# Attention of a gated cross-attention block: heads in fours, and one pipeline over all batches

## The chip, the core and the metric

The kernel runs on one core of one Trainium2 chip. Its engines work side by side, each on its own queue of instructions in order, and wait for one another through semaphores: TensorE (PE in the profile, its weight loads PEld), VectorE (DVE), ScalarE (ACT), GpSimd (POOL), and SyncE (SP), which here only issues DMAs. Matmuls write into PSUM, which has eight banks of 128 x 2 KB here; DVE and ACT read them out into SBUF. The metric is the device time of the whole program in microseconds. Where a profile is shown, its own execution's time is named, since times differ by some tenths of a per cent from run to run.

## The reference

Inputs are x and a context ctx, each of 8 batches x 256 rows x 512 columns in fp32, a mask (8 x 256 x 256, all zeros in these inputs, but added all the same), two scalar gates and the weights. Cut to what matters:

```python
def w8a8_linear(x, w, b):                  # rows of x and of w rounded to whole numbers of +-127
    qx, sx = dyn_quant(x); qw, sw = quant_weight(w)
    return einsum('bnc,oc->bno', qx, qw) * (sx * sw) + b

def xattn(x, cond, mask):                  # 16 heads of 32 columns
    q = heads(w8a8_linear(x, wq, bq)); k = heads(cond @ wk.T + bk); v = heads(cond @ wv.T + bv)
    scores = einsum('bhnd,bhld->bhnl', q, k) / sqrt(32) + mask
    o = einsum('bhnl,bhld->bhnd', softmax(scores), v)
    return w8a8_linear(concat(o), wo, bo)

x = x + tanh(g_xattn) * xattn(layernorm(x), ctx, mask)
x = x + tanh(g_ffn) * ffn(layernorm(x))    # fp8 gate, up (1408 wide) and down, columns reordered by two lists
```

The FFN rounds its weights and its input rows to an fp8 grid, after the columns are picked by a list of indices; a column that the list leaves out does not count for the row's largest value.

## The kernel before, in words

Rows lie on the 128 partitions: a batch has 2 tiles of 128 rows (TPB = 2), 2 tiles of context rows (LC = 2), and the 512 columns are 4 blocks of 128 (KC = 4), each of which holds 4 heads of 32 (HPC = 4).

Start: weights wk and wv are transposed (prep_fp32), wq and wo rounded and transposed (prep_int8), batch 0 is normalised and its q, k and v are made. mark_held writes two tables in DRAM (which columns the lists hold) by a chain of DMAs on POOL; load_held (L337) reads them back as mu_b and md_b.

The attention part, lines 187 to 762, runs batch by batch. For batch b, `attention` (L499) walks 11 steps over the batch's 8 pairs of heads:

- scores(i) (L518): for the pair (2i, 2i+1) four matmuls of 32 x 128 by 32 x 256 (two row tiles x two heads, L525), issued so that the heads alternate. A head's 32 rows of q and k lie on partitions 0, 32, 64 or 96 on, so the two heads use two row groups of TensorE's array. Each fp32 matmul stands in the profile as two passes. The results fill the tile s, two banks, of which there is one (ps_s, bufs=1). Then DVE adds the mask, turns the sign and takes the row minimum (L540, sn and nm), and ACT takes the exponential with its row sum (L550, pr).
- transposed(i) (L560), one step later: each head's pr is transposed by four matmuls against the identity (L566) into the tile t (one bank, ps_t, bufs=2), which DVE (even heads, L575) or ACT (odd heads, L573) copies out as pT.
- weighted and normalised (L578, L596), after every second pair: pT times v for four heads, in four column groups (L584, tile poT, ps_o, one bank), ACT's copy oT (L598), two transposes (L601, po), and the division by the row sums on DVE (L607).

Besides these, `attention` is given a list of other steps, handed out evenly over its 11 steps in the order of the list: for batch 0 the layer norm's statistics of the other 14 row tiles (norm_steps) and out_scales; for the others first the last batch's project_out (L630: absmax of o, rounding, transposes, matmuls with wo at L654, x updated on POOL at L665 and L666) and quantise_x2 (L670: the FFN's input rounded, transposed to x2T, and stored to DRAM on SP, L693); then the next batch's project_kv (L406: context transposed to cT, keys L424, values L438) and project_q (L452); then its share of the 29 weight pieces (prep_up L344: an indirect load on POOL, a multiplication by mu_b on POOL at L352, an absmax on DVE, rounding, transposes; prep_down; and the gathers by index). All these take their PSUM banks from a third pool (ps_m, three banks, helper `bank`). load_batch (L398) issues the next batch's context and mask loads on SP.

The order on each engine is not the order of the code. A scheduler at compile time plays the program through with modelled durations: each engine takes, among the instructions that are ready in its model, the one that stands first in the program. The order that comes out is fixed; on the chip each engine then works through its queue in order. So where a step is handed out sets its rank, not its place, and an instruction whose inputs come later than in the model holds up all behind it on its engine. A tile is allocated when a buffer of its tag is free.

After batch 7 its project_out and quantise_x2 follow alone, and then the FFN over 16 row tiles (from L766), which the change does not touch.

Of the kernel before, what the change touches and what calls it, by code (L numbers as in the profile page):

```python
# [29 lines left out]
F32 = mybir.dt.float32  # L30
BF16 = mybir.dt.bfloat16
# [9 lines left out]
P = 128  # L41
# [10 lines left out]
def tile_flamingo_block(  # L52
# [26 lines left out]
    H = 16  # L79
# [6 lines left out]
    HPC = P // D  # L86
    ISD = float(1.0 / (D ** 0.5))
# [98 lines left out]
    with ExitStack() as actx:  # L186
# [8 lines left out]
        ps_t = actx.enter_context(tc.tile_pool(name="ps_t", bufs=2, space=PSUM))  # L195
        ps_o = actx.enter_context(tc.tile_pool(name="ps_o", bufs=1, space=PSUM))
        ps_m = actx.enter_context(tc.tile_pool(name="ps_m", bufs=3, space=PSUM))

        def bank(name, dt=F32):
            n = 512 if dt == F32 else 1024  # L200
            return ps_m.tile([P, n], dt, tag="m", name=name)
# [204 lines left out]
        def project_kv(b, cr):  # L406
            cT = ld.tile([P, KC, L], F32, tag="cT", name=f"cT_{b}", bufs=1)
            kT = kv.tile([P, KC, L], F32, tag="kT", name=f"kT_{b}")
            v = kv.tile([P, LC, C], F32, tag="v", name=f"v_{b}")
# [25 lines left out]
            def values(lt):  # L435
                pv = bank(f"pv_{b}_{lt}")
# [8 lines left out]
                nc.vector.tensor_tensor(v[:, lt, :], pv, bv_b, ALU.add)  # L445
# [53 lines left out]
        def attention(b, qT, kT, v, mk, others):  # L499
# [8 lines left out]
            NP = H // 2  # L508
            PPC = HPC // 2

# [7 lines left out]
            def scores(i):  # L518
                heads = (2 * i, 2 * i + 1)
                both = ps_s.tile([P, 2, TPB, L], F32, tag="s", name=f"s_{b}_{i}")  # L520
                pss = {h: both[:, h % 2] for h in heads}

                def product(nt, h):
                    oc, r0 = h // HPC, (h % HPC) * D
# [9 lines left out]
                for h in heads:  # L534
                    sn = at.tile([P, TPB, L], F32, tag="sn", name=f"sn_{b}_{h}")
                    pr = at.tile([P, TPB, L], F32, tag="pr", name=f"pr_{b}_{h}", bufs=4)
# [23 lines left out]
            def transposed(i):  # L560
                for h in (2 * i, 2 * i + 1):
                    pr = probs.pop(h)
                    pst = ps_t.tile([P, LC, S], F32, tag="t", name=f"t_{b}_{h}")
# [14 lines left out]
            def weighted(oc):  # L578
                heads = range((oc + 1) * HPC - 1, oc * HPC - 1, -1)
                poT[oc] = ps_o.tile([P, S], F32, tag="o", name=f"poT_{b}_{oc}")  # L580

                def product(lc, h):
# [3 lines left out]
                        v[:, lc, h * D : (h + 1) * D],  # L586
# [9 lines left out]
            def normalised(oc):  # L596
                oT = at.tile([P, S], F32, tag="oT", name=f"oT_{b}_{oc}")
# [16 lines left out]
            last = NP + 2  # L614
            given = 0
            for i in range(last + 1):
                if i < NP:
                    scores(i)
                if 0 <= i - 1 < NP:
                    transposed(i - 1)  # L620
                if 0 <= i - 2 < NP and (i - 2) % PPC == PPC - 1:
                    weighted((i - 2) // PPC)
                    normalised((i - 2) // PPC)
                upto = len(others) * (i + 1) // (last + 1)
                for f in others[given:upto]:
                    f()
                given = upto
            return o
# [41 lines left out]
        def quantise_x2(b):  # L670

            xT = at.tile([P, KC, S], BF16, tag="x2T", name=f"x2T_{b}")
# [29 lines left out]
        rows_q = load_rows("q", wq, "pr", 4)  # L702
# [36 lines left out]
        start = norm_steps(TPB, NT) + [out_scales]  # L739
# [195 lines left out]
```

## Time and profile before

| | us |
|---|---|
| time, median of 3 runs | 778.96 (775.64 to 783.07) |
| the profiled execution's own time | 773.38 |
| its span (first to last instruction) | 771.6 |
| PE busy / DVE / ACT / POOL | 580.6 / 534.6 / 417.8 / 278.0 |
| first scores of batch 0; of batch 1; last scores of batch 7 | 35.5; 123.2; ends 514.3 |
| mean granted TensorE clock | 0.855 |

How to read the profile: "busy" is the time in which an engine had at least one instruction at work. A group is all instructions of one line, engine and tile; its columns are the number, the time that they cover, the mean of one, and the idle time of the engine just ahead of them with what ended it. A name like s<-kT,qT is output and inputs by the program's names. The granted clock is the share of full speed that TensorE got; it is either 1.0 or 0.5 at any one time, so a mean of 0.8 is 40% of the time at half speed. A wait for several things is put down to the one that came last. Times of a stretch are in us from the span's start.

### The profile page before, as it was taken

The numbers are of one execution on the slowest core, as the hardware profiler recorded it, in microseconds if no ns is written. First come the engines' busy times: TensorE is split into PE (matmuls) and PEld (weight loads), VectorE is DVE, ScalarE is ACT, GpSimd is POOL, SyncE is SP. The second block draws the span as 40 slices with busy tenths as digits, with TensorE's granted clock in tenths as the row PEclk, the third lists the DMA queues.
The fourth block names the chain that finished last, engine by engine and source line by source line (L and its number), as shares of the span: only waits on it lengthen the run. The fifth ranks groups of instructions, "written<-read, shape, count | busy, mean of one in ns | idle before, by whom it ended". The sixth has DMA issues, their size and how long they took to land. (4 is left out here: it accounts for less than half of the span.)

```text
span 771.6 us, 10456 instructions
## 1 busy us (share of the span) xinstructions
PE 580.6 (75%) x3584; PEld 364.4 (47%) x3584; DVE 534.6 (69%) x1421; ACT 417.8 (54%) x965; POOL 278.0 (36%) x241
## 2 busy tenths in 40 slices
PE   3852697797897797897898896765577768678762
PEld 3631465464555465654565564442354334344431
DVE  2953867957848748858857768865477777868971
ACT  3532954756756656765855666643244444445550
POOL 3623342152132242142114100060654666555440
PEclk9985888999899799799897797595698899989985
DMA  9811041030113130120114011230100101000000
GB/s 289 274 11 14 6 139 28 3 93 15 42 51 108 49 96 15 41 66 5 42 28 147 4 52 41 76 111 14 55 11 18 41 28 38 31 28 28 29 14 27
DMA packets 27157, 42.59 MB, mean 55 GB/s; under 512 B 6528, under 2 KB 14080, under 8 KB 27104
## 3 DMA queue, kind: packets, MB, share of 16 engines
q1 hardware_dynamic: 18656, 29.17, 11.2%
q0 software_dynamic: 4864, 12.22, 5.9%
q10 hardware_dynamic: 3584, 0.54, 0.4%
q8 instruction: 28, 0.46, 0.2%
q14 instruction: 25, 0.20, 0.1%
HBM read 31.28 MB, written 10.63 MB: 54 GB/s over the span
## 5 line engine op out<-in xcount | busy, mean ns | idle before, releaser
L550 ACT ACTIVATE pr<-sn,nm 128x256 f32<-128x256 f32 x256 | 127.6, 501 | 82.6 <-DVE nm L540 81.9
L525 PE MATMUL s<-kT,qT 32*128 32x256 f32 x512 | 88.5, 471 | 57.2 <-DVE nm L540 52.2
L540 DVE CUSTOM_DVE_ANT_0 sn<-s,mk 128x256 f32<-128x256 f32 x256 | 97.0, 418 | 14.4 <-PE s L525 14.4
L566 PE MATMUL t<-ident,pr 128*128 128x128 f32 x512 | 93.8, 323 | 15.9 <-DVE mv L679 6.7
L525 PEld LDWEIGHTS s<-kT,qT 32*128 32x128 f32 x512 | 52.9, 221 | 85.2 <-DVE nm L540 53.8
L566 PEld LDWEIGHTS t<-ident,pr 128*128 128x128 f32 x512 | 67.7, 164 | 43.9 <-ACT pr L550 22.1
L825 PEld LDWEIGHTS <-xg 128*128 128x128 bf16 x512 | 52.7, 104 | 74.6 <-issue 34.7
L857 POOL TENSOR_TENSOR tt<-up,sl 128x704 f32<-128x704 f32 x32 | 62.9, 1966 | 39.5 <-DVE up L847 23.8
L825 PE MATMUL p_up<-upT,xg 128*128 128x352 bf16 x256 | 52.0, 341 | 20.9 <-DVE up L847 18.2
L424 PE MATMUL pk<-cT,wkT 128*128 128x256 f32 x256 | 60.1, 391 | 3.2 <-ACT cT L417 3.0
L825 PE MATMUL p_gate<-gateT,xg 128*128 128x352 bf16 x256 | 48.9, 335 | 14.2 <-DVE gs L838 7.5
L665 POOL TENSOR_TENSOR x_sb<-x_sb,bo_b 128x512 f32<-128x512 f32 x16 | 22.4, 1406 | 97.8 <-ACT xq L462 97.8
L438 PE MATMUL pv<-wvT,cT 128*128 128x512 f32 x128 | 56.5, 594 | 0.0
L424 PEld LDWEIGHTS pk<-cT,wkT 128*128 128x128 f32 x256 | 48.8, 195 | 12.1 <-ACT cT L417 5.8
L666 POOL TENSOR_TENSOR x_sb<-x_sb,y 128x512 f32<-128x512 f32 x16 | 20.1, 1267 | 89.4 <-DVE y L662 89.3
L184 DVE TENSOR_REDUCE mxt<-tt 128x1 f32<-128x1408 f32 x16 | 25.9, 1620 | 33.6 <-POOL tt L857 33.6
L550 ACT ACTIVATION_READ_ACCUMULATOR pr<-sn,nm 128x1 f32 x256 | 48.7, 190 | 0.0
L493 POOL TENSOR_SCALAR qT<-qT,bq_c 128x256 f32<-128x256 f32 x32 | 19.4, 618 | 80.1 <-DVE qT L490 80.0
L875 PE MATMUL yp<-wdT,qtT 128*128 128x512 bf16 x176 | 44.7, 408 | 2.9 <-ACT qtT L872 2.9
L872 ACT COPY qtT<-ptq 128x1024 bf16<-128x1024 bf16 (+1 forms) x32 | 22.3, 749 | 43.0 <-PE ptq L869 43.0
L162 ACT ACTIVATE v_t<-tt,rs_t 128x1408 f32<-128x1408 f32 x16 | 23.5, 1469 | 39.9 <-DVE sy L879 39.9
L575 DVE COPY pT<-t 128x512 f32<-128x512 f32 x64 | 43.7, 682 | 1.6 <-PE t L566 1.0
(184 smaller groups left out, 1183.6 us busy)
## 6 DMA issues: line engine op xcount, KB each, us to landing
cr<-in_ctx_dram SPq DMA_DIRECT2D x8, 512.0 KB, 3.8
x_sb<-in_x_dram SPq DMA_DIRECT2D x8, 512.0 KB, 9.0
out_dram<-yo SPq DMA_DIRECT2D x16, 256.0 KB, 2.0
wd<-in_L_ffn_w_down_dram SPq DMA_DIRECT2D x4, 704.0 KB, 4.1
mk<-in_mask_BxSxS_ff_dram SPq DMA_DIRECT2D x8, 256.0 KB, 2.7
scr_x<-x2T SPq DMA_DIRECT2D x8, 256.0 KB, 3.1
scr_gate<-gateT SPq DMA_DIRECT2D x1, 1408.0 KB, 5.5
scr_up<-upT SPq DMA_DIRECT2D x1, 1408.0 KB, 5.1
```

Of the source, the lines that this page charges most:

```text
L162: nc.scalar.activation(v, src, AF.Identity, scale=rs)
L184: nc.vector.tensor_reduce(dst, src, AX.X, ALU.max, apply_absolute_value=True)
L424: nc.tensor.matmul(pk[:, :L], wTf["k"][:, cc, oc * P : (oc + 1) * P], cT[:, cc, :], start=(cc == 0), stop=(cc == KC - 1),)
L438: nc.tensor.matmul(pv, cT[:, cc, lt * P : (lt + 1) * P], wTf["v"][:, cc, :], start=(cc == 0), stop=(cc == KC - 1),)
L525: return nc.tensor.matmul(pss[h][:, nt, :], qT[r0 : r0 + D, oc, nt * P : (nt + 1) * P], kT[r0 : r0 + D, oc, :], start=True, stop=True,)
L540: nc.vector.tensor_tensor_reduce(out=sn[:, nt, :], in0=pss[h][:, nt, :], in1=mk[:, nt, :], scale=-1.0, scalar=3.0e38, op0=ALU.add, op1=ALU ...
L550: nc.scalar.activation(pr[:, nt, :], sn[:, nt, :], AF.Exp, bias=nm[:, nt : nt + 1], scale=-1.0, accum_out=sums[:, nt, h : h + 1],)
L566: nc.tensor.transpose(pst[:, lc, nt * P : (nt + 1) * P], pr[:, nt, lc * P : (lc + 1) * P], ident,)
L575: nc.vector.tensor_copy(pT, pst)
L825: nc.tensor.matmul(ph[n][:, j, :QI], xg[:, k, nt * P : (nt + 1) * P], wT[n][:, k, c0 : c0 + QI], start=(k == 0), stop=(k == KC - 1),)
L857: nc.gpsimd.tensor_tensor(tt[:, cols], up, sl, ALU.mult)
L875: nc.tensor.matmul(py, qT[:, k, :], wdT[:, k, :], start=(k == 0), stop=(k == IC - 1))
```

## The change

Three things are changed in the attention part.

1. scores works on four heads at a time. For even i it issues the eight matmuls of one column block, heads in turn (four row groups), into one tile s of four banks, of which there is again one; then the eight row minima and exponentials. For odd i it does nothing. pr gets six buffers instead of four.
2. ps_t, ps_o and ps_m become one pool of four banks, from which t, poT, po and all other steps take theirs.
3. The walk over steps leaves `attention`, which now returns its three stages. One loop runs over all 64 pairs, with the pairs' transposes one pair later and the products two pairs later also across the border of two batches. The other steps of a batch are put into eight slots, one per pair, by kind: `spread` divides each list over a stretch of slots. v's tile is allocated at its first use; oT and x2T move to a pool with one buffer.

The core of the diff (where a tile's pool alone changes, and where v becomes a list of one, is left out):

```diff
-        ps_t = actx.enter_context(tc.tile_pool(name="ps_t", bufs=2, space=PSUM))
-        ps_o = actx.enter_context(tc.tile_pool(name="ps_o", bufs=1, space=PSUM))
-        ps_m = actx.enter_context(tc.tile_pool(name="ps_m", bufs=3, space=PSUM))
+        ps_m = actx.enter_context(tc.tile_pool(name="ps_m", bufs=4, space=PSUM))
...
             def scores(i):
-                heads = (2 * i, 2 * i + 1)
-                both = ps_s.tile([P, 2, TPB, L], F32, tag="s", name=f"s_{b}_{i}")
-                pss = {h: both[:, h % 2] for h in heads}
+                if i % PPC:
+                    return
+                oc = i // PPC
+                heads = range(oc * HPC, (oc + 1) * HPC)
+                four = ps_s.tile([P, HPC, TPB, L], F32, tag="s", name=f"s_{b}_{oc}")
+                pss = {h: four[:, h % HPC] for h in heads}
...
-                    pr = at.tile([P, TPB, L], F32, tag="pr", name=f"pr_{b}_{h}", bufs=4)
+                    pr = at.tile([P, TPB, L], F32, tag="pr", name=f"pr_{b}_{h}", bufs=6)
...
-                    pst = ps_t.tile([P, LC, S], F32, tag="t", name=f"t_{b}_{h}")
+                    pst = bank(f"t_{b}_{h}").rearrange("p (c n) -> p c n", n=S)
...
-                poT[oc] = ps_o.tile([P, S], F32, tag="o", name=f"poT_{b}_{oc}")
+                poT[oc] = bank(f"poT_{b}_{oc}")[:, :S]
...
-            last = NP + 2
-            given = 0
-            for i in range(last + 1):
-                if i < NP:
-                    scores(i)
-                if 0 <= i - 1 < NP:
-                    transposed(i - 1)
-                if 0 <= i - 2 < NP and (i - 2) % PPC == PPC - 1:
-                    weighted((i - 2) // PPC)
-                    normalised((i - 2) // PPC)
-                upto = len(others) * (i + 1) // (last + 1)
-                for f in others[given:upto]:
-                    f()
-                given = upto
-            return o
+            def products(i):
+                if i % PPC == PPC - 1:
+                    weighted(i // PPC)
+                    normalised(i // PPC)
+
+            return o, (scores, transposed, products)
...
-        after = start
-        for b in range(B):
-            n0, n1 = (len(pieces) * i // (B - 1) for i in (b, b + 1))
-            others = after + pieces[n0:n1]
-            if b + 1 < B:
-                cr, mk_next = load_batch(b + 1)
-                kT_next, v_next, kv_steps = project_kv(b + 1, cr)
-                qT_next, q_steps = project_q(b + 1)
-                others = after + kv_steps + q_steps + pieces[n0:n1]
-            o = attention(b, qT, kT, v, mk, others)
-            after = project_out(b, o) + quantise_x2(b)
-            if b + 1 < B:
-                qT, kT, v, mk = qT_next, kT_next, v_next, mk_next
-        for f in after:
-            f()
+        def spread(slots, steps, first, end):
+            for k, f in enumerate(steps):
+                slots[first + k * (end - first) // len(steps)].append(f)
+
+        parts = {}
+        for g in range(B * NP + NP):
+            b, i = divmod(g, NP)
+            if i == 0:
+                slots = [[] for _ in range(NP)]
+                if b < B:
+                    o, parts[b] = attention(b, qT, kT, v, mk)
+                if b == 0:
+                    spread(slots, norm_steps(TPB, NT), 0, 4)
+                    spread(slots, [out_scales], 5, 6)
+                if b + 1 < B:
+                    cr, mk = load_batch(b + 1)
+                    kT, v, kv_steps = project_kv(b + 1, cr)
+                    qT, q_steps = project_q(b + 1)
+                    spread(slots, kv_steps, 0, 6)
+                    spread(slots, q_steps, 4 if b == 0 else 3, 7)
+                if b > 0:
+                    spread(slots, project_out(b - 1, o_last) + quantise_x2(b - 1), 2, NP)
+                if b < B - 1:
+                    n0, n1 = (len(pieces) * k // (B - 1) for k in (b, b + 1))
+                    spread(slots, pieces[n0:n1], 4 if b == 0 else 0, NP)
+                o_last = o
+            for lag in range(3):
+                if 0 <= g - lag < B * NP:
+                    parts[(g - lag) // NP][lag]((g - lag) % NP)
+            for f in slots[i]:
+                f()
```

More of the change, by code (lines that the diff above doesn't have):

```diff
@@ L86, in tile_flamingo_block @@
     HPC = P // D
+    NP = H // 2
+    PPC = HPC // 2
     ISD = float(1.0 / (D ** 0.5))
@@ L408, in project_kv @@
             kT = kv.tile([P, KC, L], F32, tag="kT", name=f"kT_{b}")
-            v = kv.tile([P, LC, C], F32, tag="v", name=f"v_{b}")
+            v = []
             def transposed(lt):
@@ L435, in values @@
             def values(lt):
+                if lt == 0:
+                    v.append(kv.tile([P, LC, C], F32, tag="v", name=f"v_{b}"))
                 pv = bank(f"pv_{b}_{lt}")
@@ L444, in values @@
                     )
-                nc.vector.tensor_tensor(v[:, lt, :], pv, bv_b, ALU.add)
+                nc.vector.tensor_tensor(v[0][:, lt, :], pv, bv_b, ALU.add)
             steps = [partial(transposed, lt) for lt in range(LC)]
@@ L497, in project_q, with attention @@
             return qT, [rows] + [partial(queries, oc) for oc in range(KC)]
-        def attention(b, qT, kT, v, mk, others):
+        def attention(b, qT, kT, v, mk):
             o = kv.tile([P, TPB, C], F32, tag="o", name=f"o_{b}")
@@ L507, in attention @@
             probs, probsT, poT = {}, {}, {}
-            NP = H // 2
-            PPC = HPC // 2
             def in_turn(products):
@@ L518, in scores @@
             def scores(i):
-                heads = (2 * i, 2 * i + 1)
-                both = ps_s.tile([P, 2, TPB, L], F32, tag="s", name=f"s_{b}_{i}")
-                pss = {h: both[:, h % 2] for h in heads}
+                if i % PPC:
[4 more added lines that the diff above has]
+                pss = {h: four[:, h % HPC] for h in heads}
                 def product(nt, h):
-                    oc, r0 = h // HPC, (h % HPC) * D
+                    r0 = (h % HPC) * D
                     return nc.tensor.matmul(
@@ L585, in product @@
                         poT[oc][r0 : r0 + D, :],
-                        v[:, lc, h * D : (h + 1) * D],
+                        v[0][:, lc, h * D : (h + 1) * D],
                         probsT[h][:, lc, :],
@@ L596, in normalised @@
             def normalised(oc):
-                oT = at.tile([P, S], F32, tag="oT", name=f"oT_{b}_{oc}")
+                oT = one.tile([P, S], F32, tag="oT", name=f"oT_{b}_{oc}")
                 nc.scalar.copy(oT, poT.pop(oc))
@@ L670, in quantise_x2 @@
         def quantise_x2(b):
-            xT = at.tile([P, KC, S], BF16, tag="x2T", name=f"x2T_{b}")
+            xT = one.tile([P, KC, S], BF16, tag="x2T", name=f"x2T_{b}")
             def rows(nt):
@@ L701, in tile_flamingo_block @@
         rows_v = load_rows("v", wv, "pT", 6)
-        rows_q = load_rows("q", wq, "pr", 4)
+        rows_q = load_rows("q", wq, "pr", 6)
         two = one.tile([P, 2, C], F32, tag="wd", name="wr_o01")
@@ L738, in tile_flamingo_block @@
         so_b = wp.tile([P, C], F32, tag="so_b", name="so_b")
-        start = norm_steps(TPB, NT) + [out_scales]
         pieces = [partial(prep_up, "gate", w_gate, k) for k in range(IC)]
```

## The prediction

> **What bounds the kernel now.** I read the page first, then the time by stage, then who waits for whom, then single stretches in order of time. The page names the costliest groups; columns after the bar are busy time, mean ns of one, then idle time of the engine just before.
>
> ```profile
> PE 580.6 (75%) x3584; PEld 364.4 (47%) x3584; DVE 534.6 (69%) x1421; ACT 417.8 (54%) x965; POOL 278.0 (36%) x241
> ...
> L550 ACT ACTIVATE pr<-sn,nm 128x256 f32<-128x256 f32 x256 | 127.6, 501 | 82.6 <-DVE nm L540 81.9
> L525 PE MATMUL s<-kT,qT 32*128 32x256 f32 x512 | 88.5, 471 | 57.2 <-DVE nm L540 52.2
> L540 DVE CUSTOM_DVE_ANT_0 sn<-s,mk 128x256 f32<-128x256 f32 x256 | 97.0, 418 | 14.4 <-PE s L525 14.4
> ```
>
> 75% for PE is an average. By the starts of the score matmuls (L525) the eight batches begin at 35.5, 123.2, 179.4, 236.1, 295.1, 351.5, 407.4 and 469.1 us, and the last scores end at 514.3; then comes a tail, and the FFN from about 545. Batches 1 to 6 take 345.9 us, 57.65 each. I cut each of them in two and asked for the busy time by stretch (columns: stretch, length, busy of PE, PEld, DVE, ACT, POOL with counts, granted clock, DMA share, GB/s):
>
> ```profile
> 179.40:206.00 26.60, 19.87 (x136) 12.22 (x132) 21.89 (x73) 16.31 (x48) 4.40 (x4) 0.81 0.00 1
> 206.00:236.10 30.10, 29.03 (x194) 19.53 (x193) 18.24 (x66) 19.62 (x55) 10.58 (x11) 1.00 0.20 62
> ...
> 295.10:322.00 26.90, 21.83 (x141) 13.52 (x138) 22.54 (x77) 16.89 (x48) 4.40 (x4) 0.75 0.00 1
> 322.00:351.50 29.50, 28.36 (x190) 18.95 (x187) 18.83 (x66) 20.13 (x56) 12.77 (x13) 1.00 0.24 72
> ```
>
> Every batch has a first half in which DVE is the fuller engine (over the six: DVE 142 of 173 us, PE 131, at granted clocks of 0.72 to 0.87), because the steps given first are the last batch's output projection and x2 quantising; and a second half that is PE alone (166 of 173 us, DVE 105), because the k, v and q projections of the next batch come there in one lump. So PE bounds half of each batch, and an alternation of PE and DVE the other half. In full-clock time a batch's PE work is about 44.4 us: in the first halves the mean clock of 0.80 means 69 of 173 us at half speed, PE busy through most of them, so some 30 of its 131 us are lost to it: (131 - 30 + 166) / 6. DVE has 247 / 6 = 41.2 us, ACT 36.5.
>
> Batch 0 is longer, 87.8 us, for one wait:
>
> ```profile
> PE s L525 <- DVE nm L540: 52.2, 22, 22.4
> ...
> DVE mx_gate L184 <- POOL wr_gate L352: 30.4, 6, 21.3
> ```
>
> Columns: us in total, times, longest. DVE stands 21.3 us (48.8 to 70.1) at an absmax of a gate weight tile, whose multiplication by mu_b on POOL waits for the table of held indices; the scores behind it on DVE wait too, so PE's 22.4 us is the same stall. Without it PE's wait for nm is 29.8 us over 21 times.
>
> **Part 1: four heads in turn.** How much a row group costs is seen where other matmuls run side by side (start, length):
>
> ```profile
> 213.36 1.07 PE L584 MATMUL poT<-pT,v 128*32 128x256 f32 x16
> 214.36 1.13 PE L525 MATMUL s<-kT,qT 32*128 32x256 f32 x8
> 215.48 0.44 PE L601 MATMUL po<-ident,oT 128*128 128x128 f32 x2
> 215.76 3.62 PE L424 MATMUL pk<-cT,wkT 128*128 128x256 f32 x16
> ```
>
> A 256-column fp32 pass alone costs about 0.22 us (pk: 16 in 3.62). A pair's eight passes in two row groups take 1.13, so two run at once (0.11 each); the sixteen passes of poT, in four column groups, take 1.07. Scores of a quad are sixteen passes. Nothing in the trace shows four row groups; ends: as poT 1.07 us, no better than two groups 2.0 us (0.38 + 15 x 0.108), one after another 3.6 us. I take 1.13, nearest to poT, the one row with four parts of the array. 64 pairs x 1.13 become 32 quads x 1.13: 36 us less PE work at full clock, 44 of the 88.5 measured, 4.5 us per batch. At 2.0 it is 8 us less; at 3.6, 43 us more. PE work of a batch falls to 39.9, beside DVE's 41.2: the late one after this is DVE.
>
> The wait that comes with it: the tile s keeps one buffer, now of four banks, so the next quad waits for all eight sn of this one. In batches 2 to 6 I paired first matmul and last reader of each bank: a pair holds its two for 4.2 us (write 1.4, wait 0.9, read 2.0). A quad: 1.4 + 0.9 + about 4, at ACT's pace, since sn has two buffers and exponentials follow at 0.49 us (72.50, 73.01, 73.50 in the trace). 6.3 of some 13 us per quad: it fits, priced at nothing while other work stands ahead on PE; with none, 6.3 - 4.2 = 2 us each, 64 us in all.
>
> **Part 2: four banks for all else, six before.** The same pairing over 179 to 469 us gives 633 us of holds, 2.18 banks on average; more than four are held 2% of the time, 6 us. Ends: nothing, and the second rival's price. I take nothing.
>
> **Part 3: one pipeline.** No instruction is added; the same steps are handed out over eight pair slots: k/v in slots 0 to 5, output projection and x2 in 2 to 7, q from 3, weight pieces across all, where before they came in that lumped order. PE's full half and DVE's full half then lie over each other. Floor: the larger of 39.9 and 41.2. Before, 57.65 against a largest engine of 44.4 is 77%; three engines at 36 to 41 in one stretch, with in-order queues, should not do much better: 80% of 41.2 gives 51.5 us per batch. Ends: only part 1 counts (57.65 - 4.5, or 53), and 48.5 (85%). Moved with the steps are their queues: weight pieces put an indirect load and a 1.27 us multiplication on POOL (busy 92 of 346 us in these batches), cr and mk loads and the x2T stores go through SP, where a cr load already waits up to 46 us for the last cT without anyone waiting for it; x2T and oT with one buffer wait for a store (3.1 us) and two transposes (0.44), a batch and a quad earlier. All priced at nothing; uncovered, the store costs 3 us a batch.
>
> Batches 1 to 6: 6 x 6.15 = 37 us less.
>
> **Batch 0, batch 7, tail.** Batch 0's stall has its cause in a chain of POOL DMAs that the change does not touch, so it stays; but the k, v and q work of batch 1, which now fills 101 to 123 (PE 20.6 of 22.2 us, DVE 13.9), can go beside the DVE-bound pairs (DVE 23.5 of 28.8 us at 72 to 101). DVE works 52.8 us of the 66.5 outside the stall; I take 8 of that 13.7, ends 0 and 30 (with the stall filled). Batch 7 has no next batch: DVE 38.5 of 45.2 us, so 3 of its 5.5 us of halved scores. The tail 514 to 545, the last x2 chain, and the FFN are unchanged.
>
> **Sum**: 37 + 8 + 3 = 48 us from the profiled execution's 773.4 (span 771.6), 725. The median shown is 779, 0.7% above it; scaled, **730 us**.
>
> **Rivals.**
> A, better than that: the k/v work fills the stall and the six batches reach 48.5: 55 + 20 + 3 = 78, scaled 700. For it: the clock was 1.00 in every half where PE was full but one (0.97), so denser PE may lose no clock. Against: DVE would be busy 85%.
> B, only two row groups run at once: parts 2 and 3 alone, some 54.5 per batch, 19 + 8 + 1 = 28 us less, 751.
> C, the clock: granted clock is 1.00 where PE is 96% busy, 0.66 in batch 7 at 76%. If spreading leaves PE everywhere at 80% and the clock goes to 0.80, PE needs 39.9 / 0.8 = 50, with 6 us idle 56 per batch: 18 us less, 760 to 775. Against: the half-clock stretches follow stretches of idle PE, which spreading removes. The Trainium skill, TensorE: Matmul & The Clock Gate, Part 1, says that the clock is halved by default and released by activity in a window of about 3.4 us; by that rule shorter scores could cost clock, and the trace's 0.66 in batch 7 agrees.
> D, slower: banks. A quad makes eight exponentials in a row, 4 us on ACT instead of 2, and ACT takes half of the t copies and all of cT, kT and oT. Waits of full banks double: t from 2.16 us (16 a batch), pk 1.01, poT 1.14, so a batch's holds go from 127 to 170 us. At 51.5 us that is 3.3 of four banks on average; if PE, in order, can keep only 2.7 filled, a batch takes 63: 6 x 5.3 - 11 = 21 us more, 800. It turns to slower below 2.9 banks. Against: 2.18 on average now. The Trainium skill speaks for it in TensorEngine Tiling (Array Packing), PSUM Bottleneck: tiling speeds TensorE but not PSUM's emptying, which may become the limit.
>
> **Chances.** Forecast 0.48, A 0.16, B 0.06, C 0.10 (half of it within 1%), D 0.20. A measurement of this kernel can tell about 1%, 8 us. Faster by more: 0.48 + 0.16 + 0.06 + 0.05 = 0.75; within: 0.05; slower: 0.20. The range runs from half of A, 698, to 790, which leaves out D's most and A's best.
>
> **What would show it.** Scores: 16 records in about 1.13 us, L525 near 44 us busy. Batch starts some 51 us apart; DVE over 78% busy in them, PE no longer at 96% in second halves; the stall before mx_gate still near 21 us. Wrong if score passes take 2 us or more per quad, if PE's waits before t, pk or pv name copies on ACT or DVE (D), if its wait for nm, outside the stall, rises from 30 to over 60 us, or if the clock falls under 0.85 in batches 1 to 6 (C).

## The result, and the profile after

The changed kernel takes **753.35 us** (median of 4 runs, 752.33 to 754.75) against 781.02 for the kernel before (4 runs, 775.64 to 783.25): a ratio of 0.9657 with a 95% interval of 0.9599 to 0.9714. So it is faster by 3.4%, where 730 us, 6.3% less than the median then known, was forecast. The profiled execution has a span of 751.4 us, against 771.6 before. The terms below are compared by these two spans, since only they can be cut into stages; they are 20.2 us apart, the medians 27.7, so the stages show some 7 us less than the whole gain.

The page of the changed kernel, same columns as before:

```profile
PE 525.7 (70%) x3561; PEld 341.6 (45%) x3584; DVE 548.2 (73%) x1429; ACT 415.0 (55%) x957; POOL 278.9 (37%) x241
...
L553 ACT ACTIVATE pr<-sn,nm 128x256 f32<-128x256 f32 x256 | 128.3, 505 | 58.1 <-DVE nm L543 45.4
L543 DVE CUSTOM_DVE_ANT_0 sn<-s,mk 128x256 f32<-128x256 f32 x256 | 98.4, 416 | 13.8 <-PE s L528 5.5
...
L528 PE MATMUL s<-kT,qT 32*128 32x256 f32 x512 | 41.3, 433 | 9.3 <-DVE nm L543 7.9
```

The scores (L528 now) are busy 41.3 us instead of 88.5, and TensorE's idle time ahead of them is 9.3 us instead of 57.2. ACT's idle time ahead of its exponentials is 58.1 us instead of 82.6, DVE's ahead of sn hardly less (13.8, before 14.4). On TensorE those are 47 and 48 us; the span fell by 20. Where the rest went is read from the stages. Cut at the first score matmul of each batch, the last stage ending with the first FFN matmul (us):

| | batch 0 | 1 | 2 | 3 | 4 | 5 | 6 | 7 and tail |
|---|---|---|---|---|---|---|---|---|
| before | 87.7 | 56.2 | 56.7 | 59.0 | 56.4 | 55.9 | 61.7 | 75.0 |
| after | 80.5 | 49.3 | 52.0 | 52.9 | 51.3 | 50.4 | 63.6 | 86.7 |

At the start of batch 6 the changed kernel is 35 us ahead. It gives 1.9 back in batch 6 and 11.7 behind it. The busy time by stretch of the changed kernel, batches 1, 5 and 6, then batch 7 up to its last scores, then the tail (columns as in the prediction; batches 2 to 4 are like 5):

```profile
116.30:165.60 49.30, 36.50 (x294) 25.42 (x294) 41.64 (x131) 31.57 (x90) 18.11 (x17) 0.93 0.14 42
...
321.80:372.20 50.40, 41.91 (x327) 28.37 (x324) 43.06 (x145) 36.25 (x101) 12.40 (x12) 0.94 0.14 44
372.20:435.80 63.60, 45.41 (x320) 31.79 (x318) 53.07 (x151) 43.42 (x114) 11.65 (x12) 0.85 0.23 75
435.80:486.00 50.20, 36.18 (x275) 23.86 (x276) 31.05 (x101) 26.32 (x81) 13.42 (x15) 0.77 0.21 64
486.00:522.50 36.50, 13.92 (x88) 8.08 (x87) 20.43 (x63) 11.30 (x29) 5.11 (x5) 0.70 0.03 10
```

Batches 1 to 5 have one pattern: DVE is the fullest engine (81 to 85% of the stretch), PE a little under it, the clock at 0.91 to 0.94. Batch 6 has 10 us more of DVE than its neighbours, and 63.60 - 53.07 = 10.5 us without DVE, about as many as they have (7.3 to 10.0). After it the engines are emptier: DVE 62% in batch 7, 56% in the tail.

Two stretches of the trace show what is in the two places. First DVE in batch 6, the lines that take the absmax of a row tile of w_down (start, length):

```profile
372.79 1.61 DVE L186 TENSOR_REDUCE mx_d<-wd 128x1 f32<-128x1408 f32 x1
...
396.89 1.61 DVE L186 TENSOR_REDUCE mx_d<-wd 128x1 f32<-128x1408 f32 x1
...
411.12 1.61 DVE L186 TENSOR_REDUCE mx_d<-wd 128x1 f32<-128x1408 f32 x1
...
428.44 1.61 DVE L186 TENSOR_REDUCE mx_d<-wd 128x1 f32<-128x1408 f32 x1
```

All four prep_down pieces, the last of the 29 but for a gather, have their absmax in batch 6. Before the change the absmaxes stood at 435.9, 456.8, 475.3 and 487.3 us: two in batch 6 (407 to 469), two in batch 7. Then TensorE at the end of batch 7, in order of time (in brackets the idle time just before, and what ended it):

```profile
484.87 1.15 PE L528 MATMUL s<-kT,qT 32*128 32x256 f32 x16
...
492.10 0.61 PE L281 MATMUL tb_x<-ident_b,q 128*128 128x128 bf16 x4 [5.72 <-DVE q L169]
492.50 1.91 PE L569 MATMUL t<-ident,pr 128*128 128x128 f32 x8
...
499.81 0.61 PE L281 MATMUL tb_x<-ident_b,q 128*128 128x128 bf16 x4 [5.39 <-DVE q L169]
500.21 1.91 PE L569 MATMUL t<-ident,pr 128*128 128x128 f32 x8
```

tb_x are the x2 transposes of batch 6. They stand in TensorE's queue ahead of transposes of the last two quads, and TensorE stands 5.72 and 5.39 us for them; behind them come the last products, the projection of batch 7 and the FFN. From the last scores to the FFN it takes 36.5 us, before 29.8.

Last, the waits of the changed kernel (total, times, longest):

```profile
DVE mx_gate L186 <- POOL wr_gate L352: 24.3, 1, 24.3
PE t L569 <- DVE woT L284: 23.6, 1, 23.6
...
PE s L528 <- DVE nm L543: 7.9, 3, 3.3
...
DVE sn L543 <- PE s L528: 5.5, 7, 1.9
```

The stall of batch 0 is still there, 24.3 us (21.3 before), and TensorE's 23.6 is the same stall under another name. The wait for nm, which a quad might have made worse, is 7.9 us in all. DVE's wait for scores is 5.5 us, before 14.4.

### The profile page after: what moved, and what is told of

It reads as the page before. It is cut to its first block, busy times and chain, and to the rows that moved or that the text cites. A ratio compares the mean times of both kernels' runs of the same rounds, so it can differ in the third digit from the quotient of the medians.

```text
span 751.4 us, 10398 instructions
## 1 busy us (share of the span) xinstructions
PE 525.7 (70%) x3561; PEld 341.6 (45%) x3584; DVE 548.2 (73%) x1429; ACT 415.0 (55%) x957; POOL 278.9 (37%) x241
## 5 line engine op out<-in xcount | busy, mean ns | idle before, releaser
L553 ACT ACTIVATE pr<-sn,nm 128x256 f32<-128x256 f32 x256 | 128.3, 505 | 58.1 <-DVE nm L543 45.4
L543 DVE CUSTOM_DVE_ANT_0 sn<-s,mk 128x256 f32<-128x256 f32 x256 | 98.4, 416 | 13.8 <-PE s L528 5.5
L569 PE MATMUL t<-ident,pr 128*128 128x128 f32 x512 | 83.6, 314 | 26.6 <-DVE woT L284 23.6
L569 PEld LDWEIGHTS t<-ident,pr 128*128 128x128 f32 x512 | 69.4, 164 | 31.6 <-DVE woT L284 23.8
L424 PE MATMUL pk<-cT,wkT 128*128 128x256 f32 x256 | 64.1, 403 | 2.4 <-issue 2.4
L836 PE MATMUL p_gate<-gateT,xg 128*128 128x352 bf16 x256 | 49.2, 337 | 14.7 <-DVE gs L849 7.9
L440 PE MATMUL pv<-wvT,cT 128*128 128x512 f32 x128 | 58.6, 603 | 0.0
L424 PEld LDWEIGHTS pk<-cT,wkT 128*128 128x128 f32 x256 | 50.7, 205 | 9.7 <-issue 2.7
L528 PE MATMUL s<-kT,qT 32*128 32x256 f32 x512 | 41.3, 433 | 9.3 <-DVE nm L543 7.9
L576 ACT COPY pT<-t 128x512 f32<-128x512 f32 x64 | 37.0, 578 | 18.7 <-PE t L569 14.0
L886 PE MATMUL yp<-wdT,qtT 128*128 128x512 bf16 x161 | 42.6, 413 | 5.1 <-ACT qtT L883 3.1
L587 PE MATMUL poT<-pT,v 128*32 128x256 f32 x512 | 41.4, 450 | 2.0 <-DVE pT L578 1.0
L893 POOL TENSOR_TENSOR yo<-yo,x_sb 128x512 f32<-128x512 f32 x16 | 21.6, 1347 | 53.7 <-issue 44.3
```

The source lines that it names most:

```text
L424: nc.tensor.matmul(pk[:, :L], wTf["k"][:, cc, oc * P : (oc + 1) * P], cT[:, cc, :], start=(cc == 0), stop=(cc == KC - 1),)
L440: nc.tensor.matmul(pv, cT[:, cc, lt * P : (lt + 1) * P], wTf["v"][:, cc, :], start=(cc == 0), stop=(cc == KC - 1),)
L528: return nc.tensor.matmul(pss[h][:, nt, :], qT[r0 : r0 + D, oc, nt * P : (nt + 1) * P], kT[r0 : r0 + D, oc, :], start=True, stop=True,)
L543: nc.vector.tensor_tensor_reduce(out=sn[:, nt, :], in0=pss[h][:, nt, :], in1=mk[:, nt, :], scale=-1.0, scalar=3.0e38, op0=ALU.add, op1=ALU ...
L553: nc.scalar.activation(pr[:, nt, :], sn[:, nt, :], AF.Exp, bias=nm[:, nt : nt + 1], scale=-1.0, accum_out=sums[:, nt, h : h + 1],)
L569: nc.tensor.transpose(pst[:, lc, nt * P : (nt + 1) * P], pr[:, nt, lc * P : (lc + 1) * P], ident,)
```

## The experiments

My theory after this: halved score time and the spread order are worth some 5.6 us in each of batches 1 to 5; the end gives back 14, because work was spread to where it stands in the way. The rival: scores and the pipeline bring little each, and something else (buffers, banks, order by chance) made the gain. I first took the change apart, then priced the score time by itself, then went at the end. Two kernels repeat score matmuls, which is said there; no kernel leaves work out.

### What the parts do alone

**Part 3 without part 1.** The changed kernel with pairs of heads again, one score tile of two banks, and six banks in the common pool:

```diff
-        ps_m = actx.enter_context(tc.tile_pool(name="ps_m", bufs=4, space=PSUM))
+        ps_m = actx.enter_context(tc.tile_pool(name="ps_m", bufs=6, space=PSUM))
...
-                if i % PPC:
-                    return
                 oc = i // PPC
-                heads = range(oc * HPC, (oc + 1) * HPC)
-                four = ps_s.tile([P, HPC, TPB, L], F32, tag="s", name=f"s_{b}_{oc}")
-                pss = {h: four[:, h % HPC] for h in heads}
+                heads = (2 * i, 2 * i + 1)
+                both = ps_s.tile([P, 2, TPB, L], F32, tag="s", name=f"s_{b}_{i}")
+                pss = {h: both[:, h % 2] for h in heads}
```

> The changed kernel with its one pipeline, but scores of two heads at a time as before, into two banks, and one pool of six banks for all else: part 3 of the change with a pool of six, without the quads. If the halved score work on TensorE carries the gain (44 us of its busy time), some 25 us of it come back in the batches, where DVE is now nearly as full: 770 to 785, score matmuls near 88 us busy. If the even spreading alone carries it: 750 to 760.

Measured: 782.45 us, ratio 1.0055 (1.0024 to 1.0086). With a common pool of six banks the pipeline alone gains nothing; it is half a per cent slower. (With the three old pools it was not run.) Batches 1 to 5 take 58.6 us each, against 56.8 before. Its waits:

```profile
PE s L526 <- DVE nm L541: 37.0, 10, 22.6
...
DVE sn L541 <- PE s L526: 25.7, 25, 2.3
```

22.6 of the 37.0 are the stall of batch 0. The other line has grown: DVE waits 25 times, 25.7 us, for scores that come late behind other work on TensorE, where the changed kernel has 5.5 us and the kernel before 14.4. A pair's scores are needed twice as often as a quad's, and with one tile none can be made ahead.

**Parts 1 and 2 without part 3.** Quads and the pool of four, in the old walk batch by batch with the old order of lists:

```diff
-        def spread(slots, steps, first, end):
...
+        start = norm_steps(TPB, NT) + [out_scales]
+        after = start
+        for b in range(B):
+            n0, n1 = (len(pieces) * i // (B - 1) for i in (b, b + 1))
...
+                others = after + kv_steps + q_steps + pieces[n0:n1]
+            o = attention(b, qT, kT, v, mk, others)
```

> Quads into four banks and the pool of four banks, but the walk batch by batch with the other steps in their old list order: parts 1 and 2 without part 3. TensorE's second halves get shorter by two quads' worth, the first halves, where DVE is fuller, stay: 755 to 768. If four banks are too few where the projections come in a lump: 785 or more, with waits of TensorE for copies on ACT or DVE.

Measured: 839.06 us, ratio 1.0782 (1.0749 to 1.0815): 61 us slower than the kernel before, although TensorE has less to do (555.4 us busy against 580.6). Batches 1 to 5 take 67.3 us each at a clock of 0.80. Waits of this kernel:

```profile
PE tb_x L281 <- DVE q L169: 43.8, 13, 4.5
...
PE po L604 <- ACT oT L601: 37.9, 19, 11.3
```

These are not waits for a free bank. They are engines that stand at instructions whose inputs come later than the written order supposes. So I took the pool by itself.

**Part 2 alone.** The kernel before, with t, poT and all else in one pool of four banks instead of six banks in three pools; two banks stay empty:

```diff
-        ps_t = actx.enter_context(tc.tile_pool(name="ps_t", bufs=2, space=PSUM))
-        ps_o = actx.enter_context(tc.tile_pool(name="ps_o", bufs=1, space=PSUM))
-        ps_m = actx.enter_context(tc.tile_pool(name="ps_m", bufs=3, space=PSUM))
+        ps_m = actx.enter_context(tc.tile_pool(name="ps_m", bufs=4, space=PSUM))
```

> The kernel before with t, poT, po and all else from one pool of four banks, as in the change, and nothing else changed (two banks stay unused): part 2 alone. By the holds of before (2.18 of six banks on average, over four 2% of the time): 775 to 787. If a pool of four is what made quads in the old walk slow (839): 800 to 830.

Measured: 832.39 us, ratio 1.076 (1.0698 to 1.0823). I had priced this edit at nothing, and in the old walk it costs 58 us by the medians of one chip (774.65 for the kernel before). Three lines of its waits, then the last two of them in the kernel before:

```profile
PE s L523 <- DVE nm L538: 76.4, 29, 23.7
...
DVE pT L573 <- PE t L564: 23.4, 20, 4.1
ACT pT L571 <- PE t L564: 22.7, 31, 3.1
```

```profile
ACT pT L573 <- PE t L566: 6.3, 3, 3.2
...
DVE pT L575 <- PE t L566: 1.0, 3, 0.5
```

With two banks of its own for t, TensorE transposed ahead of the copies; ACT and DVE waited 7.3 us for it in all. In the common pool they wait 46.1. Pairing first matmul and last reader of each bank says the same from the other side: a t bank is held 4.05 us before, 2.16 of it waiting for its copy, and 1.87 us, 0.45 of it waiting, in this kernel. (These are means over batches 2 to 6.) And the banks are not full: all four are held at once about 1% of the time. So it is not four banks that the chip runs out of. The order that the planner wrote for a common pool has the transposes later on TensorE's queue, just ahead of their copies. That much the holds and waits show; why the planner writes that order was not found, and whether it comes of the sharing or of the number was not run: no kernel of the old walk has six banks in one pool.

**A pool of four under the new pipeline.** Pairs again, one score tile, pool of four, two banks empty; that is the first experiment with four banks in place of six:

```diff
...
-                four = ps_s.tile([P, HPC, TPB, L], F32, tag="s", name=f"s_{b}_{oc}")
...
+                both = ps_s.tile([P, 2, TPB, L], F32, tag="s", name=f"s_{b}_{i}")
...
```

> The one pipeline, scores of two heads at a time into one tile of two banks, and the pool of four banks; two banks stay unused. Beside the run with two such tiles (742) only the second tile is missing. If the second tile, which lets scores run ahead of DVE, is what carries the gain of that run: 780 to 800, with TensorE's and DVE's waits for each other at the scores back at 40 us or more. If the order that comes with a pool of four is what carries it: 740 to 755.

Measured: 767.47 us (760.27 to 771.20), ratio 0.9882 (0.9831 to 0.9932), between the two times that I expected. Under the pipeline four shared banks do no harm against six: the ratio is 0.017 lower, about 13 us. The step that costs 58 us in the old walk, from three pools to one, was not run in the new one.

This kernel is also the fairest price of the quads, since against the changed kernel only they are missing. The ratios are 0.9882 and 0.9657, some 17 us. Batches 1 to 5 take 55.8 us against 51.2, with 9.7 us of score matmuls in each against 4.8: the saved time shows almost in full there.

**A second score tile instead of quads.** The same, with the two empty banks given to scores:

```diff
-        ps_s = actx.enter_context(tc.tile_pool(name="ps_s", bufs=1, space=PSUM))
+        ps_s = actx.enter_context(tc.tile_pool(name="ps_s", bufs=2, space=PSUM))
```

> The one pipeline with scores of two heads at a time, but two such tiles of two banks, so that the next pair's scores need not wait for DVE, and the pool of four banks: PSUM is divided as in the changed kernel, and TensorE's score time is that of before (about 84 us against 41). If score time on TensorE is what counts: 770 to 785, as with one tile and six banks. If the buffer counts: 750 to 758.

Measured: 742.01 us, ratio 0.9589 (0.9529 to 0.9648), a span of 739.7. My expectation was wrong on both of its sides. The kernel does scores in pairs, 77.0 us of TensorE instead of 41.3, and is no slower than the one with quads. Its scores on the page, and DVE's wait for them:

```profile
L526 PE MATMUL s<-kT,qT 32*128 32x256 f32 x512 | 77.0, 420 | 3.2 <-DVE nm L541 2.9
```

```profile
DVE sn L541 <- PE s L526: 3.5, 4, 1.4
```

Against the pairs with one tile, DVE's wait for scores goes from 23.1 us to 3.5, and the ratio from 0.9882 to 0.9589: scores can now be made one pair ahead. By stage it is not better than quads everywhere: batches 1 to 5 take 52.6 us each (quads 51.2), but batch 6 takes 53.1 (63.6), since more of the prep_down work falls into batch 7 (DVE there and in the tail 63.0 us, against 51.5).

Batches 1 to 5 of these kernels side by side, mean us of one, from the one profiled execution of each:

| walk | scores | banks for all else | us |
|---|---|---|---|
| old | pairs, one tile | 2 + 1 + 3 (before) | 56.8 |
| old | pairs, one tile | 4 | 66.6 |
| old | quads | 4 | 67.3 |
| new | pairs, one tile | 6 | 58.6 |
| new | pairs, one tile | 4 | 55.8 |
| new | pairs, two tiles | 4 | 52.6 |
| new | quads | 4 (after) | 51.2 |

The two kernels with pairs and one tile in the new walk differ less than the table has it: the profiled executions took 788.20 and 760.27 us, on both sides of medians of 782.45 and 767.47. No part that was run has the gain by itself, and they don't add up: part 2 loses when alone, part 3 gains nothing. Part 1 alone was not run, since its four banks and the old six are more than the eight there are. Nor were pr's six buffers in place of four, or the single buffers of oT and x2T, which every kernel of the table has but the first two.

### Does the time of the scores count?

**Two row groups at a time.** The changed kernel, its eight score matmuls issued as one pair's four and then the other pair's four:

```diff
-                in_turn([partial(product, nt, h) for nt in range(TPB) for h in heads])
+                two = (heads[:2], heads[2:])
+                in_turn([partial(product, nt, h) for hs in two for nt in range(TPB) for h in hs])
```

> The changed kernel with one line other: the eight score matmuls of a quad are issued as two pairs one after the other, so that two row groups run at a time instead of four; banks, pool, pipeline and slots stay. The sixteen passes should take about 2.0 us instead of 1.15, 27 us more of TensorE in all. If TensorE still sets the pace of the batches: 770 to 780. If DVE sets it now: 753 to 760.

Measured: 751.55 us, ratio 0.9658 (0.9603 to 0.9714), no change. But the edit did not make the scores slower, so it says nothing on what it was to decide. Its group on the page:

```profile
L528 PE MATMUL s<-kT,qT 32*128 32x256 f32 x512 | 41.5, 437 | 9.0 <-DVE nm L544 8.0
```

41.5 us busy, 41.3 in the changed kernel. The sixteen passes of a quad take 1.16 us (1.15), and start in rounds of four (in the first quad at 0, 7, 27 and 34 ns, then from 0.32 us on), though the second pair's stand behind all of the first pair's in the program. I come back to this at the end.

**Scores made twice.** The changed kernel with every score matmul issued a second time into the same place:

```diff
-                in_turn([partial(product, nt, h) for nt in range(TPB) for h in heads])
+                in_turn([partial(product, nt, h) for nt in range(TPB) for h in heads] * 2)
```

> The changed kernel with the eight score matmuls of each quad issued twice in a row into the same tile: 1.15 us more TensorE work per quad at full clock, 37 us in all, about what the change took away; nothing else is added. If the shorter scores on TensorE are what the change gains by: 770 to 785, near the run with pairs (782). If the gain is the larger score buffer, which lets DVE and ACT run on, and TensorE has slack now: 753 to 762.

Measured: 784.16 us, ratio 1.0125 (1.0072 to 1.0179). Its scores on the page and DVE's wait for them:

```profile
L528 PE MATMUL s<-kT,qT 32*128 32x256 f32 x1024 | 73.7, 430 | 8.9 <-DVE nm L543 8.8
```

```profile
DVE sn L543 <- PE s L528: 24.9, 17, 2.7
```

L528 is busy 73.7 us instead of 41.3, and the span grows from 751.4 to 781.1: 30 us for 32. That the two sums agree so well is luck, as the stages show. Batches 0 and 1 together grow by 10 us, as some of the other steps moved from batch 1 into batch 0; batches 2 to 5 grow by 8.0 us each, for 4.4 us of score time; and batch 7 with the tail falls by 13.6, from 86.7 to 73.1, in another order of the same steps. So in batches 2 to 5 longer scores cost more than their own time. DVE now waits 24.9 us for scores instead of 5.5, and the clock there is 0.87 to 0.90 instead of 0.91 to 0.94. The first experiment, pairs in place of quads (83.9 us busy), cost some 30 us by the ratios, but 13 of these belong to its six banks.

**Scores made twice, two tiles.** The same doubling of the kernel with pairs and two tiles:

> Two score tiles of two banks each and the pool of four, with the four score matmuls of each pair issued twice in a row: 1.1 us more TensorE work per pair, some 60 us in all. If TensorE's score time is hidden once scores can run ahead: 745 to 757. If TensorE is the bound also here: 780 or more, TensorE over 620 us busy.

Measured: 804.25 us (791.60 to 806.67), ratio 1.0353 (1.0305 to 1.04). The profiled execution is the one of 791.60. In it the scores go from 77.0 to 134.1 us busy, and the span from 739.7 to 789.8: 50 us for 57. By stage, batches 0 and 1 together grow by 20.1 us for 14.8 us of score time, and batches 2 to 5 by 4.6 each for 7.1. So the whole grows by nearly all that was added, but in batches 2 to 5 a third of it is hidden in this execution. DVE's wait for scores stays short (9.3 us, before the doubling 3.5).

### What the end gives back

**Weight pieces over all eight batches**, so that batch 7 has its share and batch 6 is not the last:

```diff
-                if b < B - 1:
-                    n0, n1 = (len(pieces) * k // (B - 1) for k in (b, b + 1))
+                if b < B:
+                    n0, n1 = (len(pieces) * k // B for k in (b, b + 1))
```

> The changed kernel with the 29 weight pieces divided over eight batches instead of seven, so that most of the down weights' pieces fall into batch 7, which has no next batch to project. If the 14 us that the change gives back from batch 6 on are the down weights' DVE work in the already full batch 6: 742 to 748, batch 6 near 52 us. If they are the pipeline's end or the banks: 751 to 757.

Measured: 746.91 us, ratio 0.9613 (0.9569 to 0.9657); the span is 743.7, 7.7 less than the changed kernel's. The two intervals overlap, so the whole is not surely faster; the stage is clear. Batch 6:

```profile
372.80:424.90 52.10, 40.80 (x324) 27.95 (x324) 39.50 (x135) 34.34 (x98) 12.83 (x13) 0.97 0.20 66
```

Batch 6 takes 52.1 us with 39.5 of DVE, like the others: its 63.6 came from the pieces. But batch 7 and tail take 89.8 us (86.7), so a quarter of those 11.5 is lost again behind it.

**Batch 6's output steps early in batch 7.** project_out and quantise_x2 of batch 6 go to slots 1 to 4 of batch 7, ahead of the last quads, instead of 2 to 7:

```diff
-                    spread(slots, project_out(b - 1, o_last) + quantise_x2(b - 1), 2, NP)
+                    first, end = (1, 5) if b == B - 1 else (2, NP)
+                    spread(slots, project_out(b - 1, o_last) + quantise_x2(b - 1), first, end)
```

> The changed kernel with batch 6's output projection and x2 steps handed out in slots 1 to 4 of batch 7 instead of 2 to 7; the rest stays. If the stretch from the last scores to the FFN is 36.5 us instead of 29.8 because TensorE twice stands some 5.5 us at x2 transposes ahead of the last quad's work: 743 to 749, that stretch near 30 us. If it is the quad itself at the end of the pipeline: 752 to 757.

Measured: 739.97 us (738.48 to 740.56), ratio 0.9553 (0.9503 to 0.9603): the fastest median of all, below the time that I expected, by a change of two numbers for one batch. Its interval overlaps those of the two kernels with two tiles that are near it. Batch 7 up to the last scores, the tail, and TensorE at that place:

```profile
431.40:476.00 44.60, 30.89 (x243) 19.94 (x245) 33.86 (x111) 26.09 (x80) 14.19 (x15) 0.77 0.24 72
476.00:506.90 30.90, 15.68 (x118) 9.97 (x118) 17.23 (x54) 11.28 (x29) 4.57 (x5) 0.78 0.04 11
```

```profile
473.92 2.09 PE L528 MATMUL s<-kT,qT 32*128 32x256 f32 x16 [4.58 <-DVE nm L543]
...
478.93 0.61 PE L281 MATMUL tb_x<-ident_b,q 128*128 128x128 bf16 x4 [2.38 <-DVE q L169]
```

The x2 transposes now cost one wait of 2.38 us instead of 5.72 and 5.39, and from the last scores to the FFN it is 30.9 us, as I expected (30) and nearly as before the change (29.8). Batch 7 and tail together take 75.5 us, before the change 75.0.

Only half of the 11.2 us that the stage gains are in the tail. The other 5.6 lie ahead of the last scores, where the changed kernel has a second loss:

```profile
DVE sn L543 <- remote: 5.2, 1, 5.2
```

DVE stands 5.2 us for scores, up to 467.2 us, and "remote" says that the profile puts the end of this wait down to no instruction. The kernel with two row groups at a time has the same stand, this one has none. What it comes from is open, so the 5.6 us can't be put down to the slots.

**Both, and two tiles.** Pairs with two tiles, the pieces over eight batches, and the output steps early:

> Two score tiles of two banks and the pool of four, with both repairs: the 29 weight pieces over eight batches, and batch 6's output projection and x2 steps in slots 1 to 4 of batch 7. The three gains were 11 (tiles), 6 (pieces) and 13 us (last steps), measured singly. If they add up: 720 to 728. If the last two mend the same thing: 728 to 738.

Measured: 741.06 us, ratio 0.954 (0.9475 to 0.9604). The gains don't add up; it is no better than two tiles alone or the early output steps alone. Batch 7 starts at 414.2 us, the earliest of all kernels, and then:

```profile
414.20:512.50 98.30, 61.88 (x372) 37.51 (x370) 72.36 (x203) 50.79 (x130) 19.96 (x20) 0.69 0.18 58
```

98.3 us for the last stage, with 72.4 of DVE in it: the pieces arrive there. **And with no piece in batch 0** (`0 < b < B`, over batches 1 to 7), to take the stalling absmax out of batch 0's ranks:

> The same with the weight pieces over batches 1 to 7, none in batch 0, so that no absmax of a gate tile stands on DVE in front of scores while its input is not there. If the 24 us stall in batch 0 is lost time: 12 to 20 us less than the run beside it, batch 0 near 60 us. If the work that waits behind it only moves elsewhere: within 5 us of it.

Measured: 758.19 us (749.19 to 758.93), ratio 0.9713 (0.9637 to 0.9789), 17 us slower instead of 12 to 20 faster. The stall stays at 22.9 us. The planner works on what its model calls ready, so a piece handed out in batch 1 can still be pulled up into batch 0: the absmax that stands 22.9 us runs at 75.35 us, ahead of batch 1 (110.1). Batch 3 takes 55.1 us against 44.2 and batch 6 54.9 against 48.8, without a cause that I can name. So an edit of the ranks can move 10 to 15 us by the order that falls out, and I put no single difference of that size down to one cause unless a stage or a wait shows it.

## Why the prediction came out as it did

The sign was right, and the time lies in the range; the forecast of 730 was 23 us too low. Against the spans the sum was to give 771.6 - 48 = 723.6, and 751.4 came: 27.8 us short. By its own terms:

- **Part 1, right.** Sixteen passes were to take 1.13 us; they take 1.15, four at a time. L525 "near 44 us busy" is 41.3. Rival B, two row groups at once, is out. That the saved time counts holds in batches 1 to 5: between pairs and quads with the same pool 4.6 us of each batch for 4.9 us of scores.
- **The wait for the quad's tile, priced at nothing, right.** 7.9 us in all, where the uncovered price was 64.
- **Part 2, priced at nothing: not contradicted, and for no good reason.** In the new walk four shared banks cost nothing against six; against the three old pools it was not run. My ground was that six banks held 2.18 on average. In the old walk the same pool costs 58 us with all four full 1% of the time. Rival D had that size, and more (832 and 839 against its 800), for the wrong mechanism. In the changed kernel the holds of a batch did not rise to its 170 us: they are 99, 1.83 of four banks on average (batches 2 to 6, paired as in the prediction). The Trainium skill, TensorEngine Tiling (Array Packing), section PSUM Bottleneck, warns that PSUM's emptying may become the limit once TensorE is tiled; the trace doesn't bear that out here, DVE's wait for scores being 5.5 us and the sn instruction's mean 416 ns, as before (418).
- **Part 3, batches 1 to 5: the time right, with luck.** 51.5 us was the forecast for each, 51.2 is the mean, and DVE is the fuller engine, as forecast. But two errors cancel: DVE works 43.0 us of such a batch, not 41.2, and it is busy 84% of the time, not 80%; either alone gives 49 or 54 us. DVE's work in these batches went from 204.5 to 214.8 us; the last section shows where its instructions became longer.
- **What parts 2 and 3 bring without shorter scores, wrong.** Under rival B the prediction has 54.5 us a batch and 28 us in all for them. The kernel with scores made twice has B's 2.0 us of scores per quad at full clock; batches 1 to 5 take 56.5 us each, and it is 1.25% slower than the kernel before. The one with pairs and one tile takes 55.8 us for each and is 1.2% faster, some 9 us. So the spread order pays only where the scores don't hold DVE up, by quads or by a second tile.
- **Batch 0: right.** 8 us less forecast, 7.2 measured; the stall stayed (24.3 us), and TensorE did not fill it (rival A is out).
- **Clock, rival C: out.** 0.91 to 0.94 in batches 1 to 5 (before, 0.88 to 0.94), with TensorE busy 74 to 83%; batch 6 has 0.85, and batch 7, 72% busy, has 0.77. The Trainium skill, TensorE: Matmul & The Clock Gate, Part 1, puts the clock down to activity in a window of some 3.4 us; the drop in batch 7 and in the tail (0.70), where TensorE stands for 3 to 6 us at a time, agrees.
- **"Batches 1 to 6: 6 x 6.15", the first step that failed.** Batch 6 is not like the others: 63.6 us, 12.1 more than the sum has. I spread the pieces evenly over the batches and did not ask which are the last ones, nor that they are the longest on DVE. Before, they were handed out at the end of a lump, and two of the four down pieces slipped into batch 7, where TensorE and DVE had room. Batch 6 with its pieces over eight batches takes 52.1.
- **"The tail ... unchanged" and batch 7's 3 us, the second.** 86.7 us against 72 in the sum, 14.7 more. I had written that output projection and x2 go to slots 2 to 7, and reckoned "with in-order queues", but not followed it to the one place where the last slots are followed by nothing: there batch 6's x2 chain stands in TensorE's queue in front of the last two quads. This is shown for the tail, 6.7 us longer than before. Of the 8.1 us too much ahead of the last scores, 5.2 are the stand of DVE whose cause is open. With the steps in slots 1 to 4 the stage takes 75.5 us; with scores made twice and the steps still in slots 2 to 7 it takes 73.1, so the order that the planner makes of the slots counts too.

Of the 27.8 us short, these two steps are 26.8; batches 1 to 5 came out 1.6 better than the sum, the first batch and its start 1.1 worse, the FFN 1.4 longer. Two experiments get the two parts back one at a time (11.5 in batch 6, 11.2 behind it). Together, and with two tiles, they did not add; for quads alone both at once was not run.

Open: why the planner's order under a common pool is so much worse in the old walk; why a pool of four does better than one of six in the new; what held DVE for 5.2 us in batch 7; and what the stall in batch 0 is worth, since the one attempt did not remove it.

## What to carry to other kernels

A gain per batch multiplied by the number of batches is wrong at the ends: when work is spread evenly, ask what lands in the last round and what stands behind it in each in-order queue. A shared pool of buffers was not priced here by how many are full. What changed was how far its users ran ahead, and with it the order that the planner wrote; so try such a pool alone before adding it to a sum. And when a producer's result is waited for, a second buffer can be worth as much as halving its work: pairs in two tiles and quads in one came out within one per cent and a half of each other.

## What the hardware showed that I had not expected

**Row groups ran side by side in either order of issue.** In the program of the kernel with two row groups at a time, the matmuls stand as A B A B C D C D, a letter for a row group. If TensorE started them strictly in turn, C could not start before the second A, and a quad would take twice a pair, about 2.3 us. It took 1.16, with starts in rounds of four within 33 to 67 ns, and the group's busy time is 41.5 us (41.3 with A B C D A B C D). The trace names no row group, but it bears the order out: the first four starts of the first quad are 0, 7, 27 and 34 ns, and with A B C D A B C D they are 0, 6, 13 and 20, so C comes later by about the time of two more issues. The Trainium skill, TensorE: Matmul & The Clock Gate, Part 3: Packing small matmuls — row/col tiling, says that matmuls start and end in program order, with no reordering; read so, this trace shows otherwise for matmuls of different row groups.

**DVE's instructions grow beside POOL's.** The same DVE instructions became longer after the change. One case in the trace of the changed kernel, DVE and POOL together:

```profile
314.64 1.08 POOL L346 DMA_INDIRECT wr_up<-in_L_ffn_w_up_dram,dd_i  x1 [0.20 <-issue]
...
315.17 2.42 DVE L169 SCALAR_TENSOR_TENSOR q_up<-a_up,q_up 128x512 bf16<-128x512 fp8e4 x1
315.75 1.28 POOL L660 TENSOR_TENSOR x_sb<-x_sb,y 128x512 f32<-128x512 f32 x1
```

The median of this DVE instruction is 0.68 us; here it takes 2.42 and ends at 317.6, half a microsecond after POOL's addition to x (317.0). Four roundings of o take 1.44 us instead of 0.48 beside the other addition to x. Over all DVE instructions that a POOL instruction overlaps and that are more than 150 ns longer than the median of their group (groups of four and more), the excess is 19.0 us in the changed kernel and 4.1 before, and none is that much longer without POOL beside it; 15 of the 19 fall in batches 1 to 5, where DVE is the fullest engine. The Trainium skill, SBUF — State Buffer, Who interferes with whom, has the rule: DVE and GpSimd share one pair of ports by an exclusive lock. The trace agrees that one waits for the other, though the DVE instruction here began 0.58 us ahead of POOL's addition and was held all the same. Part 3 brings POOL's multiplications of weight pieces and its x updates beside DVE's full stretches; the prediction named the first as work on POOL and priced it at nothing. No run took these overlaps away, so what they cost in the end is not shown; the kernel with no piece in batch 0, the slower of its pair, has 31.7 us of them and its partner 21.2, but pairs with two tiles, faster than the quads, have 25.0.
